# Graph attention layer: node features two blocks at a time, bf16 splits moved into the dense sums, small transfers on another queue

## The chip, the cores and the metric

The kernel runs on one core of one Trainium2 chip. The metric is device time in microseconds (us) of one execution. A "profiled run" is the one execution of a kernel whose trace was kept, and it is one draw among four to seven timed ones. In the views PE is TensorE, PEld its weight loads, DVE is VectorE, ACT ScalarE, POOL GpSimd and SP SyncE; a q behind a name marks the issue of a transfer on that engine's queue, and L12 is line 12 of the kernel.

## The reference

Four graph layers run one after the other on 4096 nodes with 256 features and one 4096 x 4096 adjacency. Only layer 0 is touched. Cut to that layer:

```python
nf = (x @ W.T + b).reshape(N, H, C)                    # N 4096, H 8 heads, C 32
logit_parent = (nf * a[None, :, :C]).sum(-1)           # lp
logit_child  = (nf * a[None, :, C:]).sum(-1)           # lc
logits = leaky_relu(logit_parent[:, None] + logit_child[None], 0.2)
logits = where(adj[..., None] != 0, logits, 0.0)
out = einsum('ijh,jhc->ihc', softmax(logits, axis=1), nf)
x = layernorm(x + out)                                 # then layers 1 to 3
```

## The kernel before

Since exp(leaky_relu(p + c)) is exp(p)exp(c) or exp(0.2p)exp(0.2c), by the sign of p + c, the kernel never builds the softmax matrix. It works in three stages.

1. **Features.** For each of 32 blocks of 128 nodes: x is transposed, multiplied by W, and biased to `nf`. From it come the logits `lp`, `lc`, and `v` = [nf·exp(lc), nf·exp(0.2·lc)]. Two of these tiles are cut into a high and a low part (`src`, what the sums multiply). All of `v` is also cut into three bf16 parts (`gb`; this is called a split below), which go to memory as `gmd`.
2. **Dense sums.** For each of 16 pairs of row blocks and 8 groups of adjacency: load, cast on VectorE to `ar`, multiply by `src` on TensorE, store `ar` (`adjs`) and the mask `nb` (`nad`) for later. `zd` gets the result.
3. **Attention.** In two halves of four heads, with four row tiles each: ScalarE makes signs (`sg`), VectorE compares them with the mask `na` to 0/1 (`gt`), TensorE multiplies by `gm`, the bf16 parts of the half.

```python
for b in range(NB):                                    # features, NB = 32
    xT = self.transposed(ps, work, x, "xT")            # two transposes, a copy after each
    for c in range(2):
        nc.tensor.matmul(pn[:, :D + 2 * H], xT[:, c, :], w0[:, c, :], start=(c == 0), stop=(c == 1))
    # ... nf, lp, lc, lpT to lpd, exp, v on VectorE and ScalarE
    for i, t in ((0, v[:, :, 1, :]), (1, nf)):
        nc.scalar.copy(hi, t)
        nc.vector.tensor_sub(lo, t, hi.bitcast(F32))
    # ... three bf16 parts of v: ScalarE, VectorE, ScalarE, GpSimd, GpSimd
    for half in range(2):
        nc.scalar.dma_start(gmd[half, :, b], gb[...])
for b in range(NB):                                    # column total of nf, 64 matmuls
    for s in range(2):
        nc.tensor.matmul(pt[:, :W], one, src[:, b, 1, s], ...)
# ... dense sums
for half in range(2):                                  # attention
    for b in range(0, NB, 8):
        nc.scalar.dma_start(gm[:, b:b + 8], gmd[half, :, b:b + 8])
    for it in range(N // IT):
        for g in range(NB // K):
            nc.sync.dma_start(na[:, g * K:(g + 1) * K], nad[it, :, g * K:(g + 1) * K, :])
        for hh in range(H // 2):
            nc.scalar.dma_start(lpb, ...)              # logits of the row tile, broadcast
            nc.scalar.dma_start(z, ...)                # the dense sums of the row tile
            # ... 8 groups: Sign, compare, 32 matmuls each; then red, t1, t2, y
        nc.scalar.dma_start(yd[...], y)
```

## Time and profile before

The median is 5526.98 us of 3 runs (5522.69 to 5530.19) when first timed. In the profiled run (5533.4 us) the stages of layer 0 lie like this; a stage begins and ends with its own matmuls.

| stage | from | to | what bounds it |
|---|---|---|---|
| features | 11.1 | 219.2 | a chain of small steps over four engines |
| dense sums | 18.5 | 717.1 | DMA and TensorE together; the first pair runs beside the features |
| attention | 746.5 | 1723.0 | ScalarE and VectorE, with two holes where data is reloaded |
| later layers | 1723.0 | 5533.4 | not edited |

### The profile page before, as it was taken

To read this page: it belongs to the slowest core of one execution; us is meant where nothing else is said; L and a number is where in the kernel's file an instruction comes from. 1 tells how busy PE (TensorE), PEld (TensorE's weight loads), DVE (VectorE), ACT (ScalarE), POOL (GpSimd) and SP (SyncE) were. 2 spreads that over 40 slices of the span, in tenths; PEclk is the share of its full clock that TensorE was granted. 3 is DMA by queue.
4 is the path that set the end of the run, shared out by engine and by line. 5 is a ranking of instruction groups with operands and counts; after the bars stand their busy time and mean duration, and the time that the engine had idled before them with its cause. 6 is when DMAs were issued, how large, how long until landed. Compare 5 with 4: busy or idle time off the path is not lost. (4 is left out here: it accounts for less than half of the span.)

```text
span 5533.4 us, 72575 instructions
## 1 busy us (share of the span) xinstructions
PE 4416.8 (80%) x25835; PEld 3505.5 (63%) x25836; DVE 3492.3 (63%) x8321; ACT 3189.8 (58%) x6086; POOL 324.7 (6%) x519
## 2 busy tenths in 40 slices
PE   6899967767774997777778887876777777777799
PEld 4699967767774873555555555634555555555677
DVE  4322258878887233866666666429888888888422
ACT  4333369879994116655556666356776767676211
POOL 3344400000000100000000000000000000000000
PEclk7899989999997998899999999988999999998999
DMA  4599953332223681111111222141111111111476
GB/s 148 187 335 343 337 194 110 131 146 89 91 94 94 223 286 43 60 64 62 62 62 63 64 70 69 55 140 38 56 56 56 56 56 56 56 56 55 148 228 204
DMA packets 333886, 655.59 MB, mean 118 GB/s; under 512 B 73537, under 2 KB 146113, under 8 KB 324289
## 3 DMA queue, kind: packets, MB, share of 16 engines
q1 hardware_dynamic: 189824, 436.29, 24.3%
q10 hardware_dynamic: 112960, 113.79, 6.3%
q0 software_dynamic: 30720, 100.69, 4.8%
q8 instruction: 208, 3.41, 0.3%
q14 instruction: 174, 1.42, 0.1%
HBM read 490.46 MB, written 160.17 MB: 118 GB/s over the span
## 5 line engine op out<-in xcount | busy, mean ns | idle before, releaser
L1061 PE MATMUL ps_a<-X,aT 128*128 128x256 f32 x4096 | 1073.9, 420 | 554.6 <-ACT aT L1058 554.5
L1061 PEld LDWEIGHTS ps_a<-X,aT 128*128 128x128 f32 x4096 | 841.4, 211 | 784.1 <-ACT aT L1058 656.9
L249 PE MATMUL acc<-gm,gt 128*128 128x198 bf16 x8192 | 747.4, 250 | 254.2 <-DVE gt L244 242.4
L242 ACT ACTIVATE sg<-lpb,lc 128x1024 bf16<-128x1024 f32 x832 | 870.9, 1134 | 119.3 <-DVE gt L244 78.9
L249 PEld LDWEIGHTS <-gt 128*128 128x128 bf16 x8192 | 693.6, 98 | 307.9 <-DVE gt L244 284.8
L1058 ACT COPY aT<-ps_tp 128x512 f32<-128x512 f32 x512 | 281.0, 581 | 640.4 <-PE ps_tp L1056 639.9
L380 PE MATMUL pz<-src,ar 128*128 128x264 f32 x4096 | 549.1, 294 | 49.2 <-ACT src L337 31.9
L244 DVE TENSOR_TENSOR gt<-sg,na 128x4096 bf16<-128x4096 bf16 x208 | 474.1, 2285 | 164.6 <-ACT sg L242 164.6
L380 PEld LDWEIGHTS pz<-src,ar 128*128 128x128 f32 x4096 | 522.7, 194 | 70.3 <-ACT src L337 42.2
L811 ACT ACTIVATE ja<-e,nc 128x2048 bf16<-128x2048 f32 x256 | 509.3, 1989 | 0.0
L138 PE MATMUL ps_r<-XD,adj_piece 128*128 128x512 f32 x2048 | 500.0, 398 | 11.2 <-DMA adj_piece<-adjs 6.6
L138 PE MATMUL ps_adj<-XD,adj_piece 128*128 128x512 f32 x2048 | 492.2, 397 | 10.2 <-DMA adj_piece<-adjs 10.2
L138 PEld LDWEIGHTS ps_r<-XD,adj_piece 128*128 128x128 f32 x2048 | 378.9, 188 | 134.5 <-DVE h L1083 28.7
L138 PEld LDWEIGHTS ps_adj<-XD,adj_piece 128*128 128x128 f32 x2048 | 383.7, 189 | 93.0 <-DVE XD L113 10.9
L841 DVE SCALAR_TENSOR_TENSOR v<-e,c 128x4096 bf16<-128x4096 f32 x96 | 429.3, 4472 | 1.1
L947 DVE SCALAR_TENSOR_TENSOR e<-e,edge 128x256 f32<-128x256 f32 x1024 | 415.0, 478 | 2.0
L753 PE MATMUL ps_logit<-kT,q 64*128 64x512 f32 x1024 | 367.7, 662 | 55.0 <-ACT e L757 53.4
L372 ACT ACTIVATE nb<-a 128x512 bf16<-128x512 f32 x256 | 158.4, 630 | 356.9 <-DMA a<-in_adjt_dram 280.9
L901 DVE MAX8 cand<-v 128x8 f32<-128x256 f32 x1024 | 355.2, 411 | 3.1
L757 ACT ACTIVATE e<-ps_logit 128x1024 f32<-128x1024 f32 x256 | 261.8, 1030 | 99.0 <-PE ps_logit L753 96.3
L1056 PE MATMUL ps_tp<-ident,e 128*128 128x128 f32 x2048 | 270.8, 274 | 40.8 <-DVE e L947 40.8
L897 DVE SCALAR_TENSOR_TENSOR v<-e,hi 128x2048 f32<-128x2048 f32 x128 | 300.8, 2350 | 2.1
(288 smaller groups left out, 4786.4 us busy)
## 6 DMA issues: line engine op xcount, KB each, us to landing
adj_piece<-adjs SPq DMA_DIRECT2D x256, 512.0 KB, 5.3
adj_piece<-adjs SPq DMA_DIRECT2D x512, 256.0 KB, 3.2
a<-in_adjt_dram SPq DMA_DIRECT2D x256, 256.0 KB, 5.8
adjs<-ar POOLq DMA_DIRECT2D x256, 256.0 KB, 5.7
na<-nad SPq DMA_DIRECT2D x64, 1024.0 KB, 6.3
nad<-nb POOLq DMA_DIRECT2D x128, 256.0 KB, 5.1
lpb<-lpd ACTq DMA_DIRECT2D x32, 512.0 KB, 5.2
gmd<-gb ACTq DMA_DIRECT2D x64, 198.0 KB, 2.2
```

The source lines that it names most:

```text
L138: nc.tensor.matmul(ps, a[:, k, :], rhs(jc).rearrange("p s d -> p (s d)"), start=(jc == 0), stop=(jc == self.NB - 1))
L242: nc.scalar.activation(sg[:, k, :], lpb, AF.Sign, bias=lc[:, jc, h:h + 1])
L244: nc.vector.tensor_tensor(*flat, ALU.is_gt)
L249: nc.tensor.matmul(acc[:, q, :6 * C1], gt[:, k, q * P:(q + 1) * P], gm[:, jc, hh, :], start=(jc == 0 and q % 2 == 0), stop=(jc == NB - 1 a ...
L380: nc.tensor.matmul(pz[q][:, t, :W], ar[:, q, k, :], src[:, jc, t, s], start=(jc == 0 and s == 0), stop=(jc == NB - 1 and s == 1))
L753: nc.tensor.matmul(pl[:, s, :], q[s * A:(s + 1) * A, :], kT[s * A:(s + 1) * A, c * 512:(c + 1) * 512], start=True, stop=True)
L811: nc.scalar.activation(ja, e[:, s * HALF:(s + 1) * HALF], f, bias=nc1, accum_out=fs[:, i + s:i + s + 1])
L841: nc.vector.scalar_tensor_tensor(junk, e, c, e, op0=ALU.is_ge, op1=ALU.mult, accum_out=S)
L897: nc.vector.scalar_tensor_tensor(v, ec, hi, ec, op0=ALU.is_lt, op1=ALU.mult, accum_out=sb[:, s:s + 1])
L901: nc.vector.max(cand[:, 8 * j:8 * j + 8], v[:, k * 256:(k + 1) * 256])
L947: nc.vector.scalar_tensor_tensor(ec, ec, edge[:, j:j + 1], ec, op0=ALU.is_ge, op1=ALU.mult)
L1061: nc.tensor.matmul(pa[:, :D], aT[:, k * P:(k + 1) * P], X[:, jc, :], start=(jc == 0), stop=(jc == NB - 1))
```

## The change

There are three parts. Features are made for two blocks in a step: wide operations instead of pairs of narrow ones, one PSUM bank for all four transposes, and the column total's matmuls inside the step. The bf16 parts are no longer made there, but rebuilt from `src` in `factored`, which is called in the loop of the sums. In the attention `lpb`, `z` and `yd` are issued by GpSimd instead of ScalarE, and `gm` comes in eight pieces on SyncE's queue, alternating with `na`.

```diff
-                for b in range(0, NB, 8):
-                    nc.scalar.dma_start(gm[:, b:b + 8], gmd[half, :, b:b + 8])
                 for it in range(N // IT):
                     for g in range(NB // K):
                         nc.sync.dma_start(na[:, g * K:(g + 1) * K], nad[...])
+                        if it == 0:
+                            nc.sync.dma_start(gm[:, g * K:(g + 1) * K], gmd[half, :, g * K:(g + 1) * K])
 ...
-                        nc.scalar.dma_start(lpb, ...)
+                        nc.gpsimd.dma_start(lpb, ...)          # z and yd likewise
 ...
-            for b in range(NB):
+            for b in range(0, NB, 2):
+                two = slice(b, b + 2)
 ...             # four transposes into one bank, one copy xT, four feature matmuls
+                for i, t, eng in ((1, nf, nc.gpsimd), (0, v, nc.vector)):
+                    hi, lo = src[:, two, i, 0], src[:, two, i, 1]
+                    t = t.rearrange("p b h c -> p b (h c)")
+                    nc.scalar.copy(hi, t)
+                    eng.tensor_sub(lo, t, hi.bitcast(F32))
+                for q in range(2):
+                    for k in range(2):
+                        nc.tensor.matmul(pt[:, :W], one, src[:, b + q, 1, k], ...)
 ...
+            def factored(b):         # v again from src and exp(lc), then the three bf16 parts
 ...
             for b in range(0, NB, 2):                          # dense sums
+                for q in range(2):
+                    factored(b + q)
```

More of the change, by code (lines that the diff above doesn't have):

```diff
@@ L158, in layer0 @@
             dram = ctx.enter_context(tc.tile_pool(name="l0d", bufs=1, space=DRAM))
-            lp = pool.tile([P, NB, H], F32, name="lp")
-            lc = pool.tile([P, NB, H], F32, name="lc")
+            both = pool.tile([P, NB, 2, H], F32, name="both")
+            lp, lc = both[:, :, 0, :], both[:, :, 1, :]
             nlc = pool.tile([P, NB, H], F32, name="nlc")
@@ L169, in layer0 @@
             gmd = dram.tile([2, P, NB, H // 2, 6 * C1], BF16, name="gmd")
-            self.sums0(pool, lp, lc, lpd, nad, zd, gmd)
+            self.sums0(both, lpd, nad, zd, gmd)
             nc.vector.tensor_scalar_mul(nlc, lc, -1.0)
@@ L224, in layer0 @@
                         lpb = work.tile([P, IT], F32, name="lpb")
-                        nc.scalar.dma_start(lpb, bass.AP(tensor=lpd.tensor, offset=lpd.offset + h * N + it * IT,
+                        nc.gpsimd.dma_start(lpb, bass.AP(tensor=lpd.tensor, offset=lpd.offset + h * N + it * IT,
                                                          ap=[[0, P], [1, IT]]))
                         z = work.tile([P, Q, 2, C1], F32, name="z")
-                        nc.scalar.dma_start(z, zd[i0:i0 + Q, :, h].rearrange("b p s c -> p b s c"))
+                        nc.gpsimd.dma_start(z, zd[i0:i0 + Q, :, h].rearrange("b p s c -> p b s c"))
                         acc = psum.tile([P, Q, 256], F32, name="acc")
@@ L270, in layer0 @@
                         nc.vector.tensor_mul(y[:, :, hh, :], t1[:, :, :C], r.unsqueeze(2).to_broadcast([P, Q, C]))
-                    nc.scalar.dma_start(yd[i0:i0 + Q, :, half * D // 2:(half + 1) * D // 2].rearrange("b p d -> p b d"),
+                    nc.gpsimd.dma_start(yd[i0:i0 + Q, :, half * D // 2:(half + 1) * D // 2].rearrange("b p d -> p b d"),
                                         y.rearrange("p q h c -> p q (h c)"))
@@ L274, in layer0, with sums0 @@
         self.yd = yd
-    def sums0(self, pool, lp, lc, lpd, nad, zd, gmd):
+    def sums0(self, both, lpd, nad, zd, gmd):
         nc, tc, NB, D, N = self.nc, self.tc, self.NB, self.D, self.N
@@ L306, in sums0 @@
             src = wp.tile([P, NB, 2, 2, W], F32R, name="src")
-            xr = self.rows(self.x)
-            for b in range(NB):
-                x = work.tile([P, 1, D], F32, name="x", bufs=3)
-                nc.sync.dma_start(x, xr[:, b:b + 1, :])
-                xT = self.transposed(ps, work, x, "xT")
-                pn = ps.tile([P, 512], F32, name="ps_nf")
-                for c in range(2):
-                    nc.tensor.matmul(pn[:, :D + 2 * H], xT[:, c, :], w0[:, c, :], start=(c == 0), stop=(c == 1))
-                nf = work.tile([P, H, C1], F32, name="nf")
-                nc.gpsimd.memset(nf[:, :, C:], 1.0)
-                nc.vector.tensor_add(nf[:, :, :C], pn[:, :D].rearrange("p (h c) -> p h c", h=H),
-                                     b0[:, 0, :D].rearrange("p (h c) -> p h c", h=H))
-                for i, t in enumerate((lp, lc)):
-                    s = slice(D + i * H, D + (i + 1) * H)
-                    nc.vector.tensor_add(t[:, b, :], pn[:, s], b0[:, 0, s])
-                pt = ps.tile([P, 512], F32, name="ps_tp")
-                nc.tensor.transpose(pt[:H, :P], lp[:, b, :], self.ident)
-                lpT = work.tile([H, P], F32, name="lpT")
-                nc.scalar.copy(lpT, pt[:H, :P])
-                nc.scalar.dma_start(lpd[:, b * P:(b + 1) * P], lpT)
-                ex = work.tile([P, 2, H], F32, name="ex")
-                nc.scalar.activation(ex[:, 0], lc[:, b, :], AF.Exp)
-                nc.scalar.activation(ex[:, 1], lc[:, b, :], AF.Exp, scale=0.2)
-                v = work.tile([P, H, 2, C1], F32, name="v")
-                for s in range(2):
-                    nc.vector.tensor_mul(v[:, :, s, :], nf, ex[:, s].unsqueeze(2).to_broadcast([P, H, C1]))
-                for i, t in ((0, v[:, :, 1, :]), (1, nf)):
-                    hi = src[:, b, i, 0].rearrange("p (h c) -> p h c", h=H)
-                    lo = src[:, b, i, 1].rearrange("p (h c) -> p h c", h=H)
-                    nc.scalar.copy(hi, t)
-                    nc.vector.tensor_sub(lo, t, hi.bitcast(F32))
-                gb = work.tile([P, H, 3, 2 * C1], BF16, name="gb")
-                vv = v.rearrange("p h s c -> p h (s c)")
-                nc.scalar.copy(gb[:, :, 0, :], vv)
-                nc.vector.tensor_sub(vv, vv, gb[:, :, 0, :])
-                nc.scalar.copy(gb[:, :, 1, :], vv)
-                nc.gpsimd.tensor_sub(vv, vv, gb[:, :, 1, :])
-                nc.gpsimd.tensor_copy(gb[:, :, 2, :], vv)
-                for half in range(2):
-                    nc.scalar.dma_start(gmd[half, :, b], gb[:, half * H // 2:(half + 1) * H // 2].rearrange("p h s c -> p h (s c)"))
@@ L350, in sums0 @@
+            elc = wp.tile([P, NB, H], F32, name="elc")
             one = wp.tile([P, P], F32R, name="one")
@@ L352, in sums0 @@
             total = wp.tile([P, W], F32, name="total")
-            pt = ps.tile([P, 512], F32, name="ps_nf")
-            for b in range(NB):
-                for s in range(2):
-                    nc.tensor.matmul(pt[:, :W], one, src[:, b, 1, s], start=(b == 0 and s == 0),
-                                     stop=(b == NB - 1 and s == 1))
-            nc.scalar.copy(total, pt[:, :W])
+            pt = ps.tile([P, 512], F32, name="ps_sum")
+            xr = self.rows(self.x)
+            bb = b0.to_broadcast([P, 2, D + 2 * H])
@@ new lines, in sums0 @@
+            for b in range(0, NB, 2):
+                two = slice(b, b + 2)
+                x = work.tile([P, 2, D], F32, name="x", bufs=3)
+                nc.sync.dma_start(x, xr[:, two, :])
+                px = ps.tile([P, 512], F32, name="ps_tp")
+                for c in range(2):
+                    for q in range(2):
+                        at = (2 * c + q) * P
+                        nc.tensor.transpose(px[:, at:at + P], x[:, q, c * P:(c + 1) * P], self.ident)
+                xT = work.tile([P, 2, 2 * P], F32, name="xT")
+                nc.scalar.copy(xT.rearrange("p c i -> p (c i)"), px)
+                pn = psz.tile([P, 2, 512], F32, name="pz")
+                for q in range(2):
+                    for c in range(2):
+                        nc.tensor.matmul(pn[:, q, :D + 2 * H], xT[:, c, q * P:(q + 1) * P], w0[:, c, :],
+                                         start=(c == 0), stop=(c == 1))
+                nc.vector.tensor_add(both[:, two].rearrange("p b s h -> p b (s h)"), pn[:, :, D:D + 2 * H], bb[:, :, D:])
+                nf = work.tile([P, 2, H, C1], F32, name="nf")
+                nc.gpsimd.memset(nf[:, :, :, C:], 1.0)
+                for q in range(2):
+                    nc.vector.tensor_add(nf[:, q, :, :C], pn[:, q, :D].rearrange("p (h c) -> p h c", h=H),
+                                         b0[:, 0, :D].rearrange("p (h c) -> p h c", h=H))
+                pl = ps.tile([P, 512], F32, name="ps_tp")
+                for q in range(2):
+                    nc.tensor.transpose(pl[:H, q * P:(q + 1) * P], both[:, b + q, 0, :], self.ident)
+                lpT = work.tile([H, 2 * P], F32, name="lpT")
+                nc.scalar.copy(lpT, pl[:H, :2 * P])
+                nc.scalar.dma_start(lpd[:, b * P:(b + 2) * P], lpT)
+                nc.scalar.activation(elc[:, two], both[:, two, 1, :], AF.Exp)
+                ex = work.tile([P, 2, H], F32, name="ex")
+                nc.scalar.activation(ex, both[:, two, 1, :], AF.Exp, scale=0.2)
+                v = work.tile([P, 2, H, C1], F32, name="v")
+                nc.vector.tensor_mul(v, nf, ex.unsqueeze(3).to_broadcast([P, 2, H, C1]))
+                for i, t, eng in ((1, nf, nc.gpsimd), (0, v, nc.vector)):
[3 more added lines that the diff above has]
+                    eng.tensor_sub(lo, t, hi.bitcast(F32))
+                for q in range(2):
+                    for k in range(2):
+                        nc.tensor.matmul(pt[:, :W], one, src[:, b + q, 1, k], start=(b + q == 0 and k == 0),
+                                         stop=(b + q == NB - 1 and k == 1))
@@ new lines, in sums0 @@
+            nc.scalar.copy(total, pt[:, :W])
+            def factored(b):
+                v = work.tile([P, H, 2, C1], F32, name="vf")
+                part = lambda i, k: src[:, b, i, k].rearrange("p (h c) -> p h c", h=H).bitcast(F32)
+                for s, i in ((0, 1), (1, 0)):
+                    nc.vector.tensor_add(v[:, :, s, :], part(i, 0), part(i, 1))
+                nc.vector.tensor_mul(v[:, :, 0, :], v[:, :, 0, :], elc[:, b].unsqueeze(2).to_broadcast([P, H, C1]))
+                gb = work.tile([P, H, 3, 2 * C1], BF16, name="gb")
+                v = v.rearrange("p h s c -> p h (s c)")
+                nc.scalar.copy(gb[:, :, 0, :], v)
+                nc.vector.tensor_sub(v, v, gb[:, :, 0, :])
+                nc.scalar.copy(gb[:, :, 1, :], v)
+                nc.gpsimd.tensor_sub(v, v, gb[:, :, 1, :])
+                nc.gpsimd.tensor_copy(gb[:, :, 2, :], v)
+                for half in range(2):
+                    nc.scalar.dma_start(gmd[half, :, b], gb[:, half * H // 2:(half + 1) * H // 2].rearrange("p h s c -> p h (s c)"))
@@ L363, in sums0 @@
                 pz = [psz.tile([P, 2, 512], F32, name="pz") for _ in range(2)]
+                for q in range(2):
+                    factored(b + q)
                 for g in range(NB // G):
```

## The prediction

> **What bounds the kernel now.** I first read where layer 0 ends, because only layer 0 is edited: its last matmul group (L249, acc) starts at 1723 us of a span of 5533.4, so 3809 us are later layers whose code is unchanged. Then I cut layer 0 into stages and asked for the busy time of each engine in each. Columns: stretch, its length, busy us of PE, weight load, DVE, ACT, POOL with counts, granted TensorE clock, DMA share, GB/s.
>
> ```profile
> 11.00:224.00 213.00, 146.05 (x517) 101.99 (x518) 104.61 (x269) 97.33 (x304) 76.18 (x120) 0.73 0.42 136
> 224.00:718.00 494.00, 476.21 (x3868) 470.84 (x3866) 102.66 (x183) 154.51 (x268) 224.37 (x357) 1.00 0.94 332
> 718.00:746.00 28.00, 0.89 (x3) 0.59 (x3) 6.63 (x20) 7.02 (x7) 0.00 (x0) 0.55 0.83 341
> 746.00:1223.00 477.00, 373.13 (x4096) 346.46 (x4096) 411.01 (x335) 429.35 (x411) 0.00 (x0) 0.99 0.34 117
> 1223.00:1247.00 24.00, 0.57 (x5) 0.40 (x4) 7.15 (x10) 7.06 (x7) 0.00 (x0) 0.56 0.73 273
> ```
>
> Five stages, three different limits. 11 to 224 (features): nothing is full, DMA 42%, DVE and ACT below half; this is a chain of latencies. 224 to 718 (dense sums): PE 96% busy and DMA at 94% and 332 GB/s, both at the edge. 718 to 746 and 1223 to 1247: holes of TensorE ahead of each half of the attention, with DMA busy. 746 to 1223: ACT 90%, DVE 86%.
>
> The timeline inside the features shows the chain of one block (columns: start, length, engine, line, operation; in brackets the idle time before it and who ended it):
>
> ```profile
> 107.26 0.42 DVE L317 TENSOR_TENSOR nf<-ps_nf,b 128x256 f32<-128x256 f32 x1 [1.41 <-PE ps_nf L314]
> ...
> 108.84 0.81 ACTq L348 DMA_DIRECT2D gmd<-gb  x2
> ...
> 109.69 0.42 ACT L337 CAST src<-v 128x264 fp32r<-128x264 f32 x1 [1.10 <-POOL nf L316]
> ...
> 112.10 0.27 ACT L95 COPY xT<-ps_tp 128x128 f32<-128x128 f32 x1 [1.29 <-PE ps_tp L94]
> ...
> 113.58 0.42 DVE L317 TENSOR_TENSOR nf<-ps_nf,b 128x256 f32<-128x256 f32 x1 [2.19 <-PE ps_nf L314]
> ```
>
> From one nf to the next is 6.3 us (213/32 = 6.65 on average), through PE, DVE, ACT, PE again for each of two transposed halves, since one PSUM buffer serves all transposes. Note that ACT's DMA issues take its time: the cast at 109.69 starts when the two issues end (108.84 + 0.81 = 109.65).
>
> The hole at the half switch:
>
> ```profile
> 1216.54 6.98 ACTq L216 DMA_DIRECT2D gm<-gmd  x2
> ...
> 1228.28 0.38 ACTq L271 DMA_DIRECT2D yd<-y  x1
> 1228.70 0.59 ACTq L225 DMA_DIRECT2D lpb<-lpd  x1
> ...
> 1239.94 24.01 ACT L242 ACTIVATE sg<-lpb,lc 128x1024 bf16<-128x1024 f32 x23 [24.81 <-DMA lpb<-lpd]
> ...
> 1246.58 7.11 PE L249 MATMUL acc<-gm,gt 128*128 128x198 bf16 x64 [23.43 <-DVE gt L244]
> ```
>
> ACT's queue is in order. It holds the reload of gm (waits for TensorE's last reads), then the store of yd (waits for DVE), then lpb, and only behind them the next Sign activations: 24.8 us idle on ACT, 23.4 on TensorE.
>
> **What the Trainium skill says.** "DMA: Bandwidth & Descriptors", Specifications, puts HBM per core at about 358 GB/s; the trace agrees, 332 mean in the sums and 346 at most in a 50 us slice, so this stage has no room for more bytes. The same page, Issuing engines are not separate DMA queues, says that another issuing engine saves only the sequencer's time; this trace agrees where ACT is on the chain (0.81 us above), while in the attention ACT's issues cost nothing: lpb at 763.08 and z at 763.45 are issued under a running Sign, and the next one starts at 763.74 without a gap. "SBUF — State Buffer", SBUF: two separate sides, describes a port pair that DVE operations with two SBUF inputs and GpSimd lock against each other; the trace agrees: the two multiplies of L333 take 0.76 us at 108.61 and 1.60 at 102.26, where a POOL cast runs from 102.58. The change gives GpSimd more such work.
>
> **The change, part by part.**
>
> *Features.* The order of the built program shows 16 steps of two blocks with only these parts on TensorE: four transposes, four feature matmuls, two transposes of lp, four matmuls of the total. No sum matmuls are among them; before, the first pair of rows ran there (1/16 of the sums). Of the 32 bf16 splits (gb), 16 still lie in this stage, one per step; the other 16 lie beside the first 20 or so of 128 adjacency groups. One step from its first feature matmul: four matmuls at about 0.45 us (L314 x4 takes 1.7 to 1.9) 1.9; DVE both 0.15 and two nf at 0.34 apart 0.8; sometimes a part of a split before it 0.4; v, 128x528, as L343 0.71; ACT cast to src, 128x528, as L344 0.63; xT, one 128x512 copy, as L1058 0.58; then the next matmuls. That is 5.2 us; six handoffs at 0.05 to 0.1, one lpd issue 0.3 and port contention of 0.4 make about 6.2. Checks: ACT per step 0.58 + 0.3 + 2x0.2 + 2x0.63 + 2x0.63 for a split = 3.8, plus three issues at 0.3 to 0.4 = 4.9; DVE 4.7; POOL 3.0 (L345 1.12 twice, L346 0.67, a memset). Nothing exceeds 6.2, and the POOL subtraction for the total (1.12) ends about when xT does. So features take 11 + 16x6.3 = 112 us.
>
> *Sums.* Before, the total's 64 matmuls (7.7 us) ran after the features and the other 15 pairs from 229.8 to 717.4: 32.5 us a pair. Check by bytes: 4.2 MB read + 4.2 + 2.1 + 0.5 written = 11.0 MB at 337 GB/s = 32.6. After: 16 pairs, 520 us. The 16 late splits write 16x0.406 MB = 6.5 MB into a stage that is full: 19 us; I add 8 for ACT and POOL waiting on each other in order. End: 112 + 520 + 27 = 659 instead of 717.4: 58 us gained.
>
> *Attention.* lpb, z and yd leave ACT's queue, gm comes in eight pieces on SP's, alternating with na. The issues themselves save nothing (above). The half switch saves its hole: a piece of na and gm (1.05 + 0.81 MB) takes 5.5 us at 340 GB/s, the first is free about 4 us into the last head, so the eighth has landed by 3.7 + 8x5.5 + 2 = 50 us, and it is wanted at 29.7 (a head's time, 477/16) + 26 = 56. So the 24 us go. The first start gains little: the first product comes some 12 us earlier, but the eight pieces need 2 + 44 us of DMA all the same; I count 3. Together 27.
>
> Sum: 58 + 27 = 85; 5527 - 85 = 5442. The later 3809 us stay.
>
> **Rivals.** *Sums give it back.* Before, the sums of the first pair (32.5 us) were hidden beside the features; I count them. If the late splits also stall the adjacency pipeline (ACT's copy nb sits behind a gmd issue that waits for POOL, and POOL's stores behind its split), 20 groups at 6.5 instead of 4.1 us would cost 48, not 27. For it: DVE already waits 190 us for adjs stores here. Against: ACT is busy 31% and DVE 21%. It would give about 5465. *Features stay at 8 us a step* because GpSimd now holds an operation that TensorE waits for (lo of nf, then the total ahead of the next matmuls in order): 11 + 128 = 139, time 5469. Both together about 5490. *Sums are bound by PE, not DMA*, so that the added bytes hide, and a step takes 5.5: features 99, end 619 to 624, time about 5405. The 50 us slices in which PE is busy 50.00 speak for it, the DMA share of 0.96 in the same slices against. *GpSimd's descriptors come late*, as DVE blocks its port: lpb and z are fetched a head (30 us) ahead and take 5.2 and 4.3 us to land now, so even three times as long is hidden.
>
> **Range and chances.** The best guess is 5444, a little above the sum, since each hand-worked chain leaves waits out. The rivals span 5405 to 5490. Faster by over 2% needs 5416, that is 111 us: both the short step and free bytes. I give that 0.18. Slower by over 2% would need a new wait of 200 us: 0.01.
>
> **What would show it.** Features: the first long run of sum matmuls near 112 us, and steps of 6.3 us. Sums: 32.5 us a pair later on, more in the first three pairs, DMA still above 0.94. Attention: no TensorE idle above 5 us at the half switch, and 477 us per half. If lpb or gm ends long ACT waits there, the transfers did not hide; if the features end after 140 us, the chain was misread; if the sums take 570 or more, the added bytes or the in-order queues cost more than counted.

## More of the kernel before

The two rows of the costliest groups in the page of the kernel before that the change is aimed at (busy us, mean ns, then idle us of the engine just before the group and who ended it):

```profile
L249 PE MATMUL acc<-gm,gt 128*128 128x198 bf16 x8192 | 747.4, 250 | 254.2 <-DVE gt L244 242.4
L242 ACT ACTIVATE sg<-lpb,lc 128x1024 bf16<-128x1024 f32 x832 | 870.9, 1134 | 119.3 <-DVE gt L244 78.9
```

TensorE idles 254 us ahead of the attention's matmuls, most of it (242 us) in small pieces that end with VectorE's compare `gt`, which itself waits for ScalarE's signs (64 us of such waits between 750 and 1220). What is to be had is in the lower row: ScalarE, the busiest engine there, itself idles 119 us.

## The result

The median went from 5528.18 us (4 runs, 5522.69 to 5530.19) to 5471.14 us (4 runs, 5461.32 to 5479.15). The ratio is 0.9898, with a 95% interval from 0.988 to 0.9915. Here and below a ratio is the mean time of one kernel's fast runs over the mean of the other's of the same rounds, so it is not quite the ratio of the medians. The time lies inside the predicted range, and within 2% of before. The gain is 57 us where 84 were expected.

The stages of the changed kernel in the view by stretches (columns as in the prediction's first fence):

```profile
11.00:135.00 124.00, 87.11 (x279) 55.72 (x279) 86.20 (x151) 55.43 (x128) 56.23 (x67) 0.75 0.30 99
135.00:250.00 115.00, 89.73 (x648) 87.07 (x647) 56.55 (x98) 44.06 (x79) 65.92 (x89) 0.89 0.78 271
250.00:650.00 400.00, 385.74 (x3109) 380.56 (x3108) 82.39 (x146) 125.57 (x217) 183.84 (x291) 1.00 0.95 335
...
695.00:713.00 18.00, 1.40 (x10) 0.91 (x9) 7.20 (x20) 9.72 (x11) 3.06 (x4) 0.64 0.74 265
713.00:1190.00 477.00, 370.98 (x4050) 343.63 (x4051) 406.80 (x332) 431.63 (x413) 24.43 (x33) 0.98 0.34 126
1190.00:1200.00 10.00, 8.00 (x93) 7.54 (x91) 10.00 (x10) 8.97 (x9) 0.56 (x1) 1.00 1.02 423
```

Features now end at 134.8 instead of 219.2. The sums then take 560.5 us on their own, to 695.4, and begin badly: from 135 to 250 the DMA share is 0.78 and TensorE is busy 78% of the time, where later it is 96%. The attention runs from 713.0 to 1668.9. The half switch (1190 to 1200) has TensorE busy 8 of 10 us, against 0.57 of 24 before. Where the 54 us at the end of layer 0 came from:

| | before | after | gained | predicted |
|---|---|---|---|---|
| end of the sums | 717.1 | 695.4 | 22 | 58 |
| end of the sums to end of attention | 1005.9 | 973.5 | 32 | 27 |
| end of attention to end of kernel | 3810.4 | 3808.5 | 2 | 0 |

The same two rows of the page as those shown of before:

```profile
L250 PE MATMUL acc<-gm,gt 128*128 128x198 bf16 x8192 | 746.4, 250 | 223.1 <-DVE gt L245 206.8
L243 ACT ACTIVATE sg<-lpb,both 128x1024 bf16<-128x1024 f32 x832 | 870.9, 1134 | 87.7 <-DVE gt L245 86.1
```

ScalarE's busy time is the same to the digit, and its idle time is 31.6 us less: the attention's whole gain of 32 us is in this one number. The timeline at the half switch shows why:

```profile
1191.40 0.32 SPq L221 DMA_DIRECT2D gm<-gmd  x1
...
1194.12 0.32 SPq L221 DMA_DIRECT2D gm<-gmd  x1
...
1195.05 7.39 ACT L243 ACTIVATE sg<-lpb,both 128x1024 bf16<-128x1024 f32 x7 [1.03 <-DVE gt L245]
...
1195.07 2.89 PE L250 MATMUL acc<-gm,gt 128*128 128x198 bf16 x32 [0.98 <-DVE gt L245]
```

The eight pieces of `gm` are issued during the last head of the first half (1168.81 to 1194.12). The last has landed at 1208.86, in the next head, and TensorE waits only once for one of them, for 0.3 us. ScalarE goes on after 1.03 us instead of 24.81.

Now the features. A step of two blocks in the changed kernel's timeline (start, length, engine, line, operation, and in brackets the idle time before it and who ended it):

```profile
61.43 1.30 POOL L353 TENSOR_TENSOR src<-nf,src 128x528 fp32r<-128x528 f32 x1 [2.47 <-ACT src L352]
...
61.79 0.57 ACT L326 COPY xT<-ps_tp 128x512 f32<-128x512 f32 x1
...
62.78 0.62 PE L356 MATMUL ps_sum<-src,one 128*128 128x264 f32 x3 [0.99 <-POOL src L353]
...
63.24 1.99 PE L330 MATMUL pz<-w,xT 128*128 128x272 f32 x8
...
70.13 3.83 PE L330 MATMUL pz<-w,xT 128*128 128x272 f32 x8
```

There are two things to see. `xT` is ready at 62.36, but the next feature matmuls (L330) start at 63.24, behind the total's matmuls (L356), which stand ahead of them in TensorE's order and wait for GpSimd's subtraction to end at 62.73. And the same eight records of L330 take 1.99 us in one step and 3.83 in the next. The view of waits of 11 to 135 sums up the first:

```profile
PE ps_sum L356 <- POOL src L353: 15.3, 15, 1.3
```

It is 15.3 us over 15 steps, 1.0 us a step. For the second, here are TensorE's feature matmuls in the timeline, four steps on end:

```profile
94.05 2.00 PE L330 MATMUL pz<-w,xT 128*128 128x272 f32 x8
...
100.92 3.83 PE L330 MATMUL pz<-w,xT 128*128 128x272 f32 x8
...
109.35 3.79 PE L330 MATMUL pz<-w,xT 128*128 128x272 f32 x8
...
117.71 3.03 PE L330 MATMUL pz<-w,xT 128*128 128x272 f32 x8
...
124.78 2.00 PE L330 MATMUL pz<-w,xT 128*128 128x272 f32 x8
```

A step that begins with 2.00 us takes 6.87 us to the next one, those with 3.83 and 3.79 take 8.43 and 8.36, the one with 3.03 takes 7.07. The mean from 23.17 on is 7.75 us ((131.65 - 23.17) / 14), where the prediction had 6.3.

Last, the start of the sums. In the timeline around 195, with the idle times in brackets:

```profile
195.21 0.63 ACT L370 CAST gb<-vf 128x528 bf16<-128x528 f32 x1 [7.05 <-DMA gmd<-gb]
...
195.87 0.71 DVE L371 TENSOR_TENSOR vf<-vf,gb 128x528 f32<-128x528 f32 x1 [6.98 <-ACT gb L370]
...
196.50 1.62 DVE L389 CAST ar<-a 128x1024 fp32r<-128x1024 f32 x1
...
198.18 2.13 PE L400 MATMUL pz<-src,ar 128*128 128x264 f32 x8 [7.73 <-DVE ar L389]
```

ScalarE waits 7.05 us until an earlier store of a split has landed and `gb` is free, VectorE waits behind ScalarE, and the adjacency cast `ar` (L389), which has nothing to do with the split, stands behind that on VectorE. So TensorE stands still for 7.73 us.

### The profile page after: what moved, and what is told of

Its sections match the earlier page's. It is cut to its first block, busy times and chain, and to the rows that moved or that the text cites. A ratio compares the mean times of both kernels' runs of the same rounds, so it can differ in the third digit from the quotient of the medians.

```text
span 5477.4 us, 72326 instructions
## 1 busy us (share of the span) xinstructions
PE 4399.2 (80%) x25835; PEld 3498.0 (64%) x25836; DVE 3514.3 (64%) x8273; ACT 3173.8 (58%) x5958; POOL 402.0 (7%) x591
## 3 DMA queue, kind: packets, MB, share of 16 engines
q8 instruction: 208, 3.41, 0.3%
q14 instruction: 170, 1.39, 0.1%
## 5 line engine op out<-in xcount | busy, mean ns | idle before, releaser
L243 ACT ACTIVATE sg<-lpb,both 128x1024 bf16<-128x1024 f32 x832 | 870.9, 1134 | 87.7 <-DVE gt L245 86.1
L400 PE MATMUL pz<-src,ar 128*128 128x264 f32 x4096 | 518.5, 288 | 41.6 <-DVE ar L389 27.9
L400 PEld LDWEIGHTS pz<-src,ar 128*128 128x128 f32 x4096 | 510.1, 191 | 49.7 <-DVE ar L389 32.1
```

The costliest lines, as they stand in the source:

```text
L243: nc.scalar.activation(sg[:, k, :], lpb, AF.Sign, bias=lc[:, jc, h:h + 1])
L400: nc.tensor.matmul(pz[q][:, t, :W], ar[:, q, k, :], src[:, jc, t, s], start=(jc == 0 and s == 0), stop=(jc == NB - 1 and s == 1))
```

## The experiments

My theory after the result had three parts. The queue part works through `gm` alone. The features' step is long because GpSimd's subtraction stands in TensorE's order and because the fp32 matmuls run at half clock. And the sums lose about 2 us for every split left to them. The rivals are named with each run. All twelve kernels gave correct results. The summary comes first; the details follow. "Left" is how many of the 32 splits the built order leaves to the sums, "sums" is how long these take once the features have ended, and "attention" is from the end of the sums to that of the attention.

| run | median us | ratio to before | features end | left | sums | attention |
|---|---|---|---|---|---|---|
| before | 5528.18 | 1 | 219.2 | 0 | (overlapped) | 1005.9 |
| the change | 5471.14 | 0.9898 | 134.8 | 17 | 560.5 | 973.5 |
| e1_queues_only | 5494.96 | 0.9939 | 218.9 | 0 | (overlapped) | 973.3 |
| e8_gm_only | 5490.89 | 0.9935 | 215.1 | 0 | (overlapped) | 974.5 |
| e2_sums_only | 5503.83 | 0.9958 | 124.5 | 17 | 556.6 | 1005.6 |
| e3_splits_early | 5497.49 | 0.9941 | 185.3 | 2 | 525.8 | 973.2 |
| e10_early_pool | 5488.63 | 0.9928 | 171.4 | 2 | 531.1 | 973.2 |
| e11_store_pool | 5465.59 | 0.9889 | 139.7 | 12 | 542.5 | 973.7 |
| e4_lo_vector | 5451.92 | 0.9860 | 117.9 | 17 | 553.7 | 973.8 |
| e15_swap_lo | 5452.56 | 0.9863 | 120.2 | 17 | 551.3 | 973.2 |
| e5_total_late | 5462.47 | 0.9884 | 121.3 | 18 | 556.4 | 973.5 |
| e7_warm | 5456.67 | 0.9872 | 125.1 | 16 | 550.4 | 974.6 |
| e12_lo_vector_store_pool | 5451.26 | 0.9865 | 110.8 | 16 | 555.2 | 974.5 |
| e13_same_gb3 | 5447.03 | 0.9858 | 113.7 | 16 | 551.1 | 973.9 |

The times are of four runs each. The stage columns are of one profiled run each, so a few microseconds in them mean little by themselves.

### The queue part alone, and one transfer of it

e1_queues_only puts the queue part of the change into the kernel before:

```diff
-                for b in range(0, NB, 8):
-                    nc.scalar.dma_start(gm[:, b:b + 8], gmd[half, :, b:b + 8])
+                        if it == 0:
+                            nc.sync.dma_start(gm[:, g * K:(g + 1) * K], gmd[half, :, g * K:(g + 1) * K])
-                        nc.scalar.dma_start(lpb, ...)       # and z, yd
+                        nc.gpsimd.dma_start(lpb, ...)
```

> The kernel before with only the queue part of the change (gm in eight pieces on SP's queue between the na pieces; lpb, z and yd on GpSimd's). My theory, from the two traces: the queue part is worth the hole at the half switch (24 us) and 6 to 7 us at the first start, 30 to 33 us in all, so about 5495; the features and the sums stay at 717 us. Rival: with the features untouched the two parts overlap (the start gains less or more): 5480 or 5510.

It measured 5494.96 us (5491.36 to 5497.54), 32.5 us less than the 5527.46 of before in the same rounds. e8_gm_only moves `gm` and leaves `lpb`, `z` and `yd` with ScalarE (the first four lines of that diff):

> As the queues-only kernel, but lpb, z and yd stay on ACT's queue; only gm moves to SP's. My theory: ACT was held by gm's reload alone, so this has nearly all of the gain, within 5 us of the queues-only kernel (about 5497). Rival: yd and lpb in ACT's order hold the Sign activations as well, or the issues cost ACT its time (72 issues at 0.35 us = 25 us): then it is 15 us or more slower than queues-only.

It measured 5490.89 us (5488.8 to 5499.9), no slower than with all of them moved; the two intervals of the ratio overlap almost wholly (0.9922 to 0.9955 and 0.9919 to 0.9952). So the half of the title that speaks of GpSimd's queue is worth nothing that can be measured, and nothing is lost by it either. The gain is `gm` alone: once it is out of ScalarE's queue, what stands behind it is issued in time.

### The features and sums alone

e2_sums_only is the changed kernel with the queue part taken back (the reverse of the diff above).

> The changed kernel with the queue part undone: gm, lpb, z and yd on ACT's queue again. My theory: sums end near 695 us, the holes return, 22 us better than before: about 5505. If the queue part and the sums part add up, e1 and e2 together give the whole gain of 56. Rival: the parts depend on each other, and the two gains add up to 45 or less, or 65 or more.

It measured 5503.83 us (5495.94 to 5510.59), 23.6 us less than before. The two halves add up: 32.5 + 23.6 = 56.1, against 57 for the whole. This run gave a second thing that I had not asked for. In the features its instructions are those of the changed kernel, yet in the trace they end at 124.5 instead of 134.8. Its feature matmuls in the timeline:

```profile
95.60 1.99 PE L330 MATMUL pz<-w,xT 128*128 128x272 f32 x8
...
102.04 3.02 PE L330 MATMUL pz<-w,xT 128*128 128x272 f32 x8
...
109.28 2.00 PE L330 MATMUL pz<-w,xT 128*128 128x272 f32 x8
```

Here 6.44 and 7.24 us alternate, 13.68 in all, where the changed kernel had a pattern of four steps (6.87, 8.43, 8.36, 7.07; 30.73 in all). The same program thus falls into different patterns of full and half clock, worth 0.56 us a step (7.19 against 7.75 on average). A step that begins at full clock takes 6.44 here, with GpSimd's subtraction still in it (15.6 us of waits over 15 steps), and that is close to the 6.3 predicted.

### Splits back into the features

e3_splits_early calls `factored` in the loop of the features:

```diff
                         nc.tensor.matmul(pt[:, :W], one, src[:, b + q, 1, k], ...)
+                for q in range(2):
+                    factored(b + q)
 ...
                 pz = [psz.tile([P, 2, 512], F32, name="pz") for _ in range(2)]
-                for q in range(2):
-                    factored(b + q)
```

> The changed kernel, but all 32 bf16 splits are called in the loop over the features, so that 30 of them lie there and none in the first 20 adjacency groups. My theory: the sums lose all of their excess of about 41 us over 16 x 32.5 (561 to about 520), because half of that excess is waiting in order and not bytes; the features' step grows from 7.9 to 9 to 9.5 us (ACT 6.9 us and DVE 6.5 us of work a step), so they end at 155 to 165; together 10 to 20 us better than the change, 5451 to 5461. Rival 1 (only bytes): the sums lose 19 us and the features gain as much: 5470. Rival 2 (ACT or DVE in order makes the step 10.5 or more): 5480 or worse.

The sums lost 35 of their 40 us over 520, as the theory of the sums wanted. The time is a miss all the same: 5497.49 us (5495.48 to 5498.79), worse than the change and in the range of its second rival, since the step went to 11 us. Its timeline:

```profile
75.83 2.58 ACTq L330 DMA_DIRECT2D gmd<-gb  x4
...
78.45 0.63 ACT L370 CAST src<-nf 128x528 fp32r<-128x528 f32 x1 [4.14 <-POOL gb L328]
...
79.14 0.59 PE L374 MATMUL ps_sum<-src,one 128*128 128x264 f32 x1 [5.40 <-ACT src L370]
```

ScalarE's queue is in order, the stores of the split stand in it and wait for GpSimd, and the cast that TensorE needs stands behind them: 4.14 us of ScalarE, 5.40 of TensorE. I had counted engines' loads and not this order. e10_early_pool adds to it that GpSimd issues the stores:

```diff
-                    nc.scalar.dma_start(gmd[half, :, b], ...)
+                    nc.gpsimd.dma_start(gmd[half, :, b], ...)
```

> The splits-early kernel (5497) with the same stores on GpSimd's queue. My theory: its step of 11.1 us was ACT held by the issue of gmd (2.1 to 2.6 us for four issues, then 4 us idle until GpSimd is done); freed of it, the step is bound by GpSimd's work, 1.3 + 0.1 + 2 x 1.77 + 4 issues at 0.6 = 7.4, or by the chain of 7.9 to 8.5: features end at 140 to 150, sums 526: 5450 to 5465. Rival: the extra DVE and ACT work of the second split in a step is what made it 11.1: then no better than 5490.

It came to 5488.63 us (5485.7 to 5491.04), better than e3 by 9 us, but far from what was expected. Its steps are a steady 10.5 us, with the feature matmuls at half clock (662 ns a record on average, against 585 in the change). So ScalarE's queue was only part of e3's loss, and what sets 10.5 us in this kernel I did not find out. The number is that of its rival (the work of the second split in a step), but the trace does not single this out: from 80 to 122 GpSimd is busy 29.2 of 42.1 us, VectorE 25.9, ScalarE 17.9. e11_store_pool makes the same edit in the changed kernel without moving the splits:

> The changed kernel with the stores of the splits (gmd) issued on GpSimd's queue, straight behind GpSimd's own last operation of a split, instead of on ACT's. My theory: ACT's in-order wait for GpSimd (shown in the splits-early run, 2 to 4 us idle a step) and for the store's landing is what costs the sums half of their excess; the sums' first 115 us shorten by 10 to 20, the features' step by 0.5: 5445 to 5460. Rival: the stall belongs to the two gb buffers and full DMA, whoever issues: 5465 to 5471. Against both: GpSimd's queue, with about 0.6 us an issue, becomes the late one: 5475 or more.

It measured 5465.59 us (5462.25 to 5469.8). Its interval of the ratio (0.9873 to 0.9906) overlaps that of the change (0.988 to 0.9915), so it is at best a little faster: a miss for the theory, and inside the first rival's 5465 to 5471. Its sums are 18 us shorter, but the built order also did 20 splits in the features instead of 15, so this run doesn't tell the queue's effect from that of the splits.

### GpSimd in TensorE's order

e4_lo_vector changes one word: the low part of `nf` is subtracted by VectorE.

```diff
-                for i, t, eng in ((1, nf, nc.gpsimd), (0, v, nc.vector)):
+                for i, t, eng in ((1, nf, nc.vector), (0, v, nc.vector)):
```

> The changed kernel with one word changed: the low part of nf is subtracted on DVE, not GpSimd. My theory: in the changed kernel the first matmul of the total waits for ACT, the other three and the next feature matmuls behind them for this 1.3 us GpSimd subtraction (about 1.0 us idle in 15 of 16 steps in the chain of waits); on DVE it takes 0.71. So a step of 7.9 us becomes 7.2 to 7.5, the features end 6 to 12 us earlier (123 to 129), the time is 5459 to 5465. Rival: DVE is in order behind the splits' operations and TensorE waits as long for it: no change, 5471, or worse.

It measured 5451.92 us (5448.59 to 5456.54): 19 us less than the change, all of its runs below all of the change's, and better than expected. But it takes work off GpSimd as well, so a rival stood: that the load of GpSimd, or what it does to VectorE on the port that they share, is what costs. In the changed kernel VectorE's subtraction beside GpSimd's takes 1.24 us on average, in e4 0.73. The last run was made for this. e15_swap_lo swaps the two engines, so each has as much to do as in the change:

```diff
-                for i, t, eng in ((1, nf, nc.gpsimd), (0, v, nc.vector)):
+                for i, t, eng in ((1, nf, nc.vector), (0, v, nc.gpsimd)):
```

> The changed kernel with the two engines of the low parts swapped: GpSimd now subtracts for v and VectorE for nf, so each engine has as many subtractions of the same size as in the changed kernel, and only which of the two GpSimd holds is different. Theory (order: GpSimd's slow subtraction stands before the total's matmuls in TensorE's order): as in e4_lo_vector, a step of 5.7 to 6.9 us, features end at 118 to 124 us, time 5452 to 5459. Rival (the load of GpSimd, or what its use of the shared port does to VectorE, is what costs): nothing changes, a step of 7.9 us, features end at 132 to 137, time 5465 to 5472. Between them: both have a share, in the proportion measured.

It measured 5452.56 us (5447.81 to 5455.52), the same as e4. Its timeline:

```profile
62.30 0.70 DVE L353 TENSOR_TENSOR src<-nf,src 128x528 fp32r<-128x528 f32 x1
...
62.40 0.72 PE L330 MATMUL pz<-w,xT 128*128 128x272 f32 x2
...
63.05 0.64 PE L356 MATMUL ps_sum<-src,one 128*128 128x264 f32 x3
...
63.12 1.39 POOL L353 TENSOR_TENSOR src<-v,src 128x528 fp32r<-128x528 f32 x1
```

GpSimd's subtraction takes no less than before (1.39 us here, 1.53 on average), but nothing on TensorE waits for it, since `v`'s low part is first read in the sums. The built order has also put two feature records ahead of the total's last three matmuls. The rival falls: in the features GpSimd is busy 53.7 us against 55.1 in the change and VectorE 81.6 against 84.2, so the load and what the engines do to each other are nearly the same, and the time went down by 19 us. What cost was which of the two subtractions GpSimd held: TensorE's wait for the low part of `nf` is 1.5 us in all here, and was 15.3. How much of the 19 us is this wait, and how much a better pattern of the clock (next part), the runs do not separate. e2, with the wait in place, shows that a pattern alone can end the features 10 us sooner.

### The clock

e5_total_late takes the total's matmuls out of the step and runs all 64 after the features, as the kernel before did:

```diff
-            pt = ps.tile([P, 512], F32, name="ps_sum")
 ...
+            pt = ps.tile([P, 512], F32, name="ps_tp")
+            for b in range(0, NB, 2):
                 for q in range(2):
                     for k in range(2):
                         nc.tensor.matmul(pt[:, :W], one, src[:, b + q, 1, k], ...)
```

> The changed kernel with the 64 matmuls of the total after the features, in the bank of the transposes, so that TensorE waits for no subtraction inside a step. My theory: the step loses 1.0 us of waiting and about 0.8 of the four matmuls, 7.9 to 6.1 or 6.5; features end near 110; the total's 7.7 us come back at the end of them: 15 us better, 5456. Rival: with TensorE less busy its granted clock in the features falls below 0.75, more steps run their feature matmuls at 3.8 us instead of 2.0, and 8 us or less are gained: 5463 or more.

It measured 5462.47 us (5460.31 to 5466.93), between the two. The wait for GpSimd is gone, but now nearly all feature matmuls run at half clock: one of their records takes 628 ns on average, against 585 in the change and 558 in e4. Less work in a step left TensorE slower at the rest. e7_warm adds to e5 six small matmuls a step whose result is never read, to see whether that raises the clock:

```diff
+                for k in range(6):
+                    nc.tensor.matmul(pn[:, k % 2, 288:416], one, one, start=True, stop=True)
```

> The total-late kernel (5462) with six matmuls of 128 columns a step into unused columns of pn: work whose result is never read, put into TensorE's idle time after the transposes. It tests the clock: in the total-late run nearly every step ran its feature matmuls in 3.4 to 3.8 us, in the changed kernel some ran in 2.0. My theory: with TensorE busier, more of the 16 steps run at the full clock, the mean of the eight matmul records falls below 3 us, and features end up to 15 us earlier, though TensorE does more work: 5447 to 5462. Rival: the clock does not follow so small a load, and the step grows by the 0.4 to 0.7 us of the added work: 5468 to 5475.

It measured 5456.67 us (5451.98 to 5458.34), inside what the theory expected, but not for its reason: a record took 610 ns, against 628, the features ended 3.8 us later, not sooner, and the sums were 6 us shorter with two splits fewer left to them. That filler did not raise the clock to speak of. Whether another would is open.

The traces hold a hint of what goes on, found only when all runs were in. From 75 us on e15's steps begin like this:

```profile
82.42 0.90 PE L330 MATMUL pz<-w,xT 128*128 128x272 f32 x2
...
89.25 0.91 PE L330 MATMUL pz<-w,xT 128*128 128x272 f32 x2
...
96.08 0.91 PE L330 MATMUL pz<-w,xT 128*128 128x272 f32 x2
```

They are 6.83 us apart, six times on end. "TensorE: Matmul & The Clock Gate", Part 1: The HAM clock gate, in the Trainium skill says that a free-running window of 3413 ns decides between half and full clock. Twice that is 6.83. e2's pair of steps is 13.68, four windows being 13.65; the change's pattern of four steps is 30.73, nine windows being 30.72; e5's last steps take 6.82, 6.85, 6.81 and 6.85. So the step seems to settle on a multiple of that window: a shorter chain meets a slower clock and is as long as before.

The record of the clock in the traces, which I had not used, bears this out. In all fourteen it knows only full and half clock, and every stretch but the last, which the end of the run cuts, is a whole multiple of 3.41 us. In e15 it is full and half in turn from 72.6 to 120.4. Two such stretches (columns as in the prediction's first fence):

```profile
82.84:86.25 3.41, 3.41 (x11) 2.54 (x9) 2.65 (x4) 1.32 (x3) 1.69 (x3) 0.50 0.57 186
86.25:89.66 3.41, 2.13 (x11) 1.05 (x10) 2.29 (x6) 2.16 (x6) 1.78 (x3) 1.00 0.11 17
```

At half clock TensorE is busy all the 3.41 us and the next stretch is at full clock; there it is busy 2.13 us, and the next is at half clock again. It does not hold for every step: e12's steps of 5.9 us, at full clock from 74.8 to 102.1, are no multiple, nor are e10's of 10.51, which go on alike when the clock stays at half from 122 to 173. The window would also be a reason for the spread of the change's runs (18 us, against 4 for e13, most of whose steps are at full clock). That the clock alternates in step with the loop is thus seen in the traces. That it sets the loop's length is argued and not shown: no run changed the window or held the clock.

### Together

e12_lo_vector_store_pool has the edits of e4 and e11.

> The changed kernel with both edits that helped: nf's low part on DVE (alone 5452) and the gmd stores on GpSimd's queue (alone 5466). My theory: they add in different stages. The first frees GpSimd in the features, so that its stores no longer lengthen the step (features end at 115 to 120 as with the first alone), and the second takes the sums from 554 to about 542 us: layer 0's sums end near 660, time 5436 to 5443, the fastest so far. Rival: the sums' excess after an early start is bytes into a full DMA, and the gain of the stores alone came from its 20 instead of 15 early splits: then 5450.

It measured 5451.26 us (5449.04 to 5452.35): nothing is added to e4. Most steps are now 5.9 us with the matmuls at full clock, but the sums are no shorter than e4's, with 16 splits left. That speaks against the queue of the stores as e11's gain, and for the number of splits left. e13_same_gb3 gives `gb` a third buffer on top:

```diff
-                gb = work.tile([P, H, 3, 2 * C1], BF16, name="gb")
+                gb = work.tile([P, H, 3, 2 * C1], BF16, name="gb", bufs=3)
```

> The same with three buffers for a finished split (gb) in place of two. My theory: ACT's first cast of a split waits for the store of two splits before to land (16 to 23 us of such waits between 120 and 250 us); a third buffer takes most of these out: 4 to 10 us better than with two. Rival: the waits move to vf, which still has two buffers, or to full DMA: within 3 us.

It measured 5447.03 us (5444.72 to 5448.62), 4 us less than e12, with all four runs below all of e12's. This is the fastest version found: 1.4% below the kernel before and 0.4% below the change. A split that waits for an earlier store thus costs something, but little of the 31 us that the sums still lose.

## Why the prediction was right or wrong

**The bound of each stage: right, but for one of its reasons.** Once the splits were done, a pair of rows took 33.1 us at a DMA share of 0.95, where 32.5 were predicted. The 358 GB/s that the prediction took for the ceiling are none here: the loads of `gm` and `na` run at 421 GB/s for 30 us (710 to 740, DMA share 1.02). What is full in the sums, at 335 GB/s, is the time of the DMA engines. The rival in which the sums are bound by TensorE and the added bytes hide (5405 us) is out: every kernel with late splits pays for them, and the bytes are part of it (see the sums below).

**Features: the step was wrong, and it is the largest miss** (134.8 instead of 112, 23 us of it). Two terms of that sum failed.

- "four matmuls at about 0.45 us (L314 x4 takes 1.7 to 1.9) 1.9". The profile writes two records for one fp32 matmul: x128 for 64 matmuls in both kernels. The four records that I read were two matmuls, so four matmuls at the clock that I read them at are some 3.8 us. They measured 2.0, 3.0 and 3.8 in turn, by the clock granted. The 1.9 was right only for full clock, and I never asked at which clock L314 had run (615 ns a record on average, against some 0.25 us spacing at full clock: 2.00 us for eight).
- "the POOL subtraction for the total (1.12) ends about when xT does". It ended 0.4 us after `xT`, took 1.39 on average, and three total matmuls came after it before TensorE was free: a wait of 1.0 us a step, and in the step shown 0.88 us from `xT` to the feature matmuls. Both e4 and e15 remove most of it and gain 19 us. The rival of the prediction that says just this ("because GpSimd now holds an operation that TensorE waits for") names this. That its 5469 is right to 2 us is luck: it put the features' end at 139 (134.8), the loss of the sums at 27 (40.5) and the attention's gain at 27 (32).

The terms as listed also add up to 5.0 us and not 5.2, a slip too small to matter. The rest of the step was, if anything, put too high: at full clock the same program made a step in 6.44 us (e2), with the wait in it, where 6.3 had been predicted without. About 2 of the 23 us come from elsewhere: the first feature matmul starts at 13.0 and not 11. The first step took 10.2 us, which a uniform 6.3 had not allowed for either. And part of the 23 us is the profiled run's own: it is the slowest of its four (5479.15, median 5471.14), and e2's features ended 10 us earlier.

**Sums: the mechanism was right, the size too small.** The term "16 late splits ... 19 us; I add 8" was 27 and measured 40.5, or 36.6 in e2. The runs give a better rule: with 2 splits left the sums take 525.8 to 531.1, with 12 left 542.5, with 16 to 18 left 550 to 560, so about 2 us a split beside the 520. Of these, the bytes are 1.2 us (396 KB at the 335 GB/s of this stage); the rest I take to be the waiting in order that the timeline at 195 shows. The DMA share agrees with such a division in the changed kernel: 17 splits at 1.2 us are 20 us, and 115 us (135 to 250) at a share of 0.78 instead of 0.95 are 21 us of DMA time left unused, together the 40.5. It was named in the prediction as a rival with 48 us; the truth lies between.

**Attention: right, and a little too low.** The hole of the half switch was put at 24 us, and from the first head's reduction to the last the trace lost 25.6; the first start was put at 3 and gave 6.4 (first head's reduction 54.4 us after the sums' end instead of 60.9). That GpSimd's issues themselves bring nothing was said, and e8 shows it. That slow descriptors would not matter holds as well: `lpb` lands in 3.9 us from GpSimd's queue, 5.2 from ScalarE's before.

**The sum.** Predicted 58 + 27 = 85; the traces show 22 + 32 = 54. The total fell well inside the range because the rivals had been counted into it, not because the middle was good.

**Left open.** What sets e10's 10.5 us; whether the clock can be held by other means; and how much would come back if the first pair of rows ran beside the features again. The feature matmuls now use the sums' PSUM buffers, which stands against that, and no run tried it.

## What to carry to other kernels

When work is given to a slower engine, ask first which in-order queue stands behind its result: here the same two subtractions on the same two engines cost 19 us more in one assignment than in the other. Work moved out of a latency-bound stage into a full one comes back at the price of its bytes and of the waiting in order, so count both for each piece moved (2 us a split here, of which 1.2 for bytes). Before using a matmul's duration from a profile, check how many records one matmul makes and at which clock they ran.

## What the Trainium skill lacked or had wrong

- How the profile records fp32 matmuls, on no page that I read: two records for one matmul (128 for 64, in both kernels), while fp32 transposes (64 for 64) and fp32r matmuls (4096 for 4096) have one. What "FP8 and Floating Point Precision", TensorE Precision Notes, says of the cost (fp32 takes four passes) agrees: four such matmuls of 272 columns take 2.00 us at full clock, 0.50 each, and a pair of the sums has 256 fp32r matmuls of 264 columns in 33.1 us, 0.13 each.
- "TensorE: Matmul & The Clock Gate", Part 1, has the window of 3413 ns, but not that a loop of a few such windows can fall in step with it: steps of 6.83 us (e15, e5), pairs of 13.68 (e2), fours of 30.73 (the change). That the window sets these lengths is argued and not shown. The same section says that sustained activity releases the throttle; six small matmuls in a step of about 7 us did too little for that (610 against 628 ns a record).
